# A decoder on one core: norm scaling, masks and feed-forward remainders open to a second elementwise engine, the diagonals' product in one piece per chunk, the softmax reciprocals as a task of their own

## The chip, the core and the metric

The kernel runs on one core of a Trainium2 chip. A core has five instruction queues, each of which is worked off strictly in order: PE (TensorE, matrix products and transposes), DVE (VectorE) and ACT (ScalarE) for elementwise work, POOL (GpSimd), which is used here for elementwise work and fills, and SP (SyncE), which issues all transfers. The metric is the device time of one execution in microseconds (us): 819.33 us is the median of three runs before the change (817.36 to 820.14).

## What is computed

Six layers, each followed by a layer norm of its sum with its input, over 8 batches of 256 tokens with 256 features, 16 heads of 16:

```python
x = ln(x + L0_attn(x))        # gated recurrence: z, h~, associative scan, gate
x = ln(x + L0_xattn(x, ctx, mask_ik1, bias))   # scores/4 + bias, -inf where mask == 0, softmax
x = ln(x + L0_ffn(x))         # norm, 8-bit grid over ALL batches, ternary weights
x = ln(x + L1_attn(x))        # relative positions: q.rel_k[idx], p.rel_v[idx], clipped at 20
x = ln(x + L1_xattn(ctx, ctx, x, mask_bk0))    # softmax over where(mask, q.k, -1e10)/4
x = ln(x + L1_ffn(x))         # silu(gate) * up, then down, 768 hidden

def ln(x):
    m = mean(x); v = var(x)
    return (x - m) / sqrt(v + 1e-5)
```

The maximum over all batches in `L0_ffn` is a barrier: no batch passes it before all have reached it.

## The kernel before

**A planner writes the queues.** Every step of the kernel is a Python generator that yields operations to `Order.run` (L139). An operation is made by `do(engine, cost, ready, emit)`, which fixes the engine, by `either(ready, (engine, cost, emit), ...)`, which offers several, or by `dma(...)`. The planner keeps a time for each engine at which it comes free, takes the operation that could start first (within 0.1 us the more urgent one), and emits its instructions. So the order of each queue is fixed when the program is built, out of the costs in the source, and on the chip each engine goes through its queue in that order. With `either`, the way that could start earliest is taken, and with equal starts the cheaper one: `copy` (PSUM to SBUF, DVE at 0.60 or ACT at 0.47) is the common case. PE's operations carry a kind: plain ("d"), scores ("s", four heads beside each other in row groups) and values ("v", four in column groups). Going from one kind to another has a price in the plan.

**Attention.** An item is one batch in one of three attentions: `x0` (L0_xattn), `s1` (L1_attn) and `x1` (L1_xattn). An item is worked in four quads of four heads. `quad` (L896) makes scores for four heads on PE, then for each head on DVE a custom instruction that adds the bias and finds the maximum (L941, `sn`, `nm`). `head` (L952) has ACT make the exponentials with their sums (L957, `p`), PE turn them (L502, `pt`), and DVE or ACT copy them out (L291 or L292, `pts`). `values` (L980) multiplies by the values on PE (L995, `pv`). After the fourth quad `attend_out` (L1015) does the rest in one string: reciprocals of the sums on DVE (L1020, `rsum`), their spread over the features on POOL (L1026, `rsw`), a turn on PE (`ps_rs`), a copy (`oT`), and for `s1` `by_distance` (L1443); then the product with `pv` (L1041), the output projection (`pso`), the residual (L1061) and the norm.

**Distances in s1.** Scores depend on the distance through a table that is written to DRAM and read back along diagonals as `band` (L1318 to L1357); the probabilities near the diagonal go to DRAM (`pb`) and come back as `acc` (L1425), one row per distance. `by_distance` turns `acc` on PE (L1455, `psa`), copies it (`at`) and adds its product with the value table into `pv` (L1468). It does so for two chunks `c` of features and two halves `t` of the tokens, each half with a turn, a copy and a product of its own, with two `at` buffers.

**Norms.** `norm` (L527) takes statistics on DVE (L538, L540), the reciprocal root on POOL (L543 to L548, `rs_...`) and the scaling, two instructions of 128x256, on DVE (L553, `x_...` and `xn`). `settle` and `turn_x` call it and turn the result for the next layer. There are 56 such scalings: 8 of l0a, which read PSUM, and 48 that read SBUF.

**Masks.** The x0 mask becomes `neg` on DVE (L1137) and is added into the bias on POOL (L1144); the x1 mask becomes `hide` on DVE (L1585).

**The last layer.** `gated` (L1657) makes gate and up products (`fg`, `fu`) in a rounded part and a remainder; for each third of the hidden features ACT makes the tanh (L1692), DVE two products (L1696, L1703), ACT the rounded copy `h[:, 0]` (L1708), and DVE the remainder `h[:, 1]` (L1712); then come the down product (L1723, `psd`), the residual (L1733), the norm and the output transfer.

**Loads.** `loads` (L367) puts the transfers of the beginning into SP's queue: `cols` (biases and norm scales), then `xT` of batch 0, the three recurrence weights `wa`, and so on.

Of the kernel before, what the change touches and what calls it, by code (L numbers as in the profile page):

```python
# [19 lines left out]
P = 128  # L20
# [176 lines left out]
def do(engine, cost, ready, emit, kind="d"):  # L197

    needs = [x for x in ready if isinstance(x, Held) and x.i is None]
    times = [x.at if isinstance(x, Held) else x for x in ready]  # L200
    return (yield ("op", [(engine, cost, emit)], max(times), kind, needs))
# [6 lines left out]
def dma(ready, count, emit, rate=300):  # L208

    return (yield ("op", [("SP", 0.0, emit)], max(ready), (count, rate), ()))  # L210
# [6 lines left out]
def get(slots, name, at=0.0):  # L217
    ((t, i),) = yield ("get", slots, 1, at)
    return Held(slots, name).take(t, i)
# [3 lines left out]
def kernel(  # L223
# [54 lines left out]
    def on_dve(n):  # L278
        return 0.08 + n * 1.02e-3
# [87 lines left out]
    def loads():  # L367
# [6 lines left out]
        t = yield from dma([0.0], 18432, lambda: nc.sync.dma_start(out=cols, in_=cols_in))  # L374
        yield from load_xT(0)
        for i in range(3):
            events["wa", i] = yield from dma(
                [0.0], 262144, lambda: nc.sync.dma_start(out=wa[i], in_=chunked(a_w[i]))
            )
        for b in range(1, 4):  # L380
            yield from load_xT(b)
# [145 lines left out]
    def norm(y, t_y, make, name, make2=None):  # L527
# [22 lines left out]
        def scaled(make, i):  # L550
            dst = make()
            for t in range(NQ):
                nc.vector.tensor_scalar(  # L553
                    dst[:, t, :], y[:, t, :], mv[:, t, 0:1], rstd[:, i, t : t + 1], ALU.subtract,
                    ALU.mult,
                )

        t = yield from do("DVE", 0.9, [t_y], stats)
        t_r = yield from do("POOL", 0.9 if n == 1 else 1.1, [t], root)
        if n == 2:  # L560
            t_2 = yield from do("DVE", 0.66, [t_r], lambda: scaled(make2, 1))
        t = yield from do("DVE", 0.66, [t_r], lambda: scaled(make, 0))
# [389 lines left out]
    def head(it, n, j, p, s, nm, t, left, times):  # L952
# [11 lines left out]
        it.t_sums.append(t_e)  # L964
        times.append(t_e)
# [49 lines left out]
    def attend_out(it, t_pv):  # L1015

        ai, b = it.ai, it.b
# [16 lines left out]
        oT = yield from get(oT_bufs, f"oT{it.name}", t)  # L1034
        t = yield from copy([t, oT.at], oT.tile, ps.tile)
        ps.drop(t)
        if ai == 1:
            t_pv = yield from it.by_distance(t_pv)
# [79 lines left out]
    def item_x0(b):  # L1118
# [3 lines left out]
        if b > 1:  # L1122
# [13 lines left out]
            "DVE", on_dve(512), [t_m, neg.at],  # L1136
            lambda: nc.vector.tensor_scalar(  # L1137
# [119 lines left out]
    def layer1_self():  # L1257
# [5 lines left out]
        at_bufs = slots(rel, "at", 2, [P, 4, P])  # L1263
# [22 lines left out]
    def item_s1(b, kr_bufs, wide_bufs, acc_bufs, tail_bufs, at_bufs, band_bufs):  # L1286
# [90 lines left out]
        def tails_task(n, p, left, t_p):  # L1377
# [43 lines left out]
            if len(it.t_pb) in (2, 4) and n % 2 == 1:  # L1421
# [14 lines left out]
                events[it.key("acc", c)] = t_d  # L1436
                if c == 1:
                    it.pb_set.drop(t_d)
# [4 lines left out]
        def by_distance(t_pv):  # L1443
            for c in range(KC):
                t_a = yield from event(it.key("acc", c))
                for n in (2 * c, 2 * c + 1):
                    t_t = yield from event(it.key("tail", n))
                    t_a = max(t_a, t_t)
                for t in range(NQ):
                    ps = Held(banks, f"psa{b}_{t}_{c}")  # L1450
                    turned = lambda: ps.tile.rearrange("p a (j q) -> p (a j) q", q=P)

                    def emit():
                        for j in range(4):
                            nc.tensor.transpose(  # L1455
                                turned()[: 2 * NA, j, :],
                                it.acc.tile[:, c, t, 2 * j : 2 * j + 2, :].rearrange("p h r -> p (h r)"),
                                ident,
                            )

                    t_t = yield from do("PE", TURNS, [t_a, ps], emit)
                    at = yield from get(at_bufs, f"at{b}_{t}_{c}", t_t)
                    t_t = yield from copy([t_t, at.at], at.tile[: 2 * NA], turned()[: 2 * NA])
                    ps.drop(t_t)

                    def emit():
                        for j in range(4):
                            nc.tensor.matmul(  # L1468
                                it.pv.tile[32 * j : 32 * j + 32, c, t * P : (t + 1) * P],
                                drv[:, t, :],  # L1470
                                at.tile[: 2 * NA, j, :],
                                start=False,
                                stop=(t == NQ - 1 and c == KC - 1),
                                tile_position=(0, 32 * j),
                                skip_group_check=True,
                            )

                    t_pv = yield from do("PE", on_pe(256), [t_t, t_pv], emit, "v")
                    at.drop(t_pv)
            it.acc.drop(t_pv)  # L1480
            return t_pv

        it.by_distance = by_distance
# [84 lines left out]
    def item_x1(b):  # L1568
# [3 lines left out]
        if b > 0:  # L1572
# [11 lines left out]
            "DVE", on_dve(512), [t_m, hide.at],  # L1584
            lambda: nc.vector.tensor_scalar(  # L1585
# [71 lines left out]
    def gated(b, gu, dn, t_w, hT_bufs):  # L1657
# [13 lines left out]
        for i in range(NH // 2):  # L1671
            psg = Held(banks, f"fg{b}_{i}")

            def emit(ps, w):
# [35 lines left out]
            t = yield from do(  # L1710
                "DVE", on_dve(512), [t],
                lambda: nc.vector.tensor_tensor(h[:, 1], sg.tile, h[:, 0], ALU.subtract),  # L1712
# [135 lines left out]
```

## Time and profile before

| | before |
|---|---|
| median of 3 runs (range) | 819.33 us (817.36 to 820.14) |
| the profiled execution, device time | 817.66 us |
| its span, first to last instruction | 815.9 us |
| instructions | 21213 |
| matrix products on PE, weight loads | 7175, 7175 |
| mean granted TensorE clock | 0.995 |
| moved by the transfers | 77.67 MB, mean 95 GB/s |

The profile shows one execution. Its page gives the busy time of each engine, 40 slices of the span with the busy share of each engine in tenths, the chain of work that ended last, and groups of equal instructions by source line. Further views list the engines' busy time in chosen stretches ("windows"), who waited for whom, and the instructions in order of time. A PE matrix product overlaps its neighbours, so PE counts as busy while it is not at its best pace. In the order of time the stages are: the recurrence to about 60 us, x0 to about 280 us, the barrier and L0_ffn with the start of s1 to about 320 us, s1 with x1 beside it to about 690 us, and the last layer with the remaining x1 items to the end.

### The profile page before, as it was taken

To read this page: it belongs to the slowest core of one execution; us is meant where nothing else is said; L and a number is where in the kernel's file an instruction comes from. 1 tells how busy PE (TensorE), PEld (TensorE's weight loads), DVE (VectorE), ACT (ScalarE), POOL (GpSimd) and SP (SyncE) were. 2 spreads that over 40 slices of the span, in tenths; PEclk is the share of its full clock that TensorE was granted. 3 is DMA by queue.
4 is the path that set the end of the run, shared out by engine and by line. 5 is a ranking of instruction groups with operands and counts; after the bars stand their busy time and mean duration, and the time that the engine had idled before them with its cause. 6 is when DMAs were issued, how large, how long until landed. Compare 5 with 4: busy or idle time off the path is not lost.

```text
span 815.9 us, 21213 instructions
## 1 busy us (share of the span) xinstructions
PE 782.6 (96%) x7175; PEld 598.8 (73%) x7175; DVE 700.7 (86%) x2452; ACT 635.4 (78%) x2047; POOL 209.9 (26%) x398
## 2 busy tenths in 40 slices
PE   7999999999999999999999999999999999999995
PEld 6886777776777786656666777776777766799884
DVE  3899889988888698787899799899898998989985
ACT  2349988989988458896789799899899898846841
POOL 3520221121211044234333213242243322110020
PEclk9999999999999999999999999999999999999997
DMA  5735521100100449899976406645357443000001
GB/s 181 224 114 84 70 46 44 39 16 27 41 27 28 155 101 216 165 170 185 173 158 137 112 26 133 133 93 120 88 112 155 108 100 100 19 28 14 15 14 39
DMA packets 177681, 77.67 MB, mean 95 GB/s; under 512 B 155046, under 2 KB 171430, under 8 KB 177574
## 3 DMA queue, kind: packets, MB, share of 16 engines
q1 hardware_dynamic: 177574, 76.32, 41.9%
q8 instruction: 57, 0.93, 0.5%
q14 instruction: 50, 0.41, 0.2%
HBM read 41.66 MB, written 34.64 MB: 94 GB/s over the span
## 4 chain that ended last, share of the span: by engine, by line
PE 62%; DVE 13%; ACT 10%; DMA 6%; issue 4%; POOL 2%; SPq 2%; POOLq 0%; DVEq 0%; ACTq 0%
PE pt L502 14%; PE s L913 9%; PE pv L995 8%; ACT p L957 7%; PE pso L519 4%; DVE sn L941 4%; PE psv L519 4%; PE psq L508 4%; PE psk L508 3%; PE psd L1723 3%; ACT pts L292 2%; PE psa L1455 2%; DMA sk<-w 1%; PE fg L1678 1%; PE psr L1308 1%
## 5 line engine op out<-in xcount | busy, mean ns | idle before, releaser
L957 ACT ACTIVATE p<-sn,nm 128x256 f32<-128x256 f32 x768 | 381.3, 507 | 23.9 <-DVE nm L941 18.4
L502 PE MATMUL pt<-ident,p 128*128 128x128 f32 x1536 | 207.1, 277 | 5.2 <-ACT p L957 2.1
L502 PEld LDWEIGHTS pt<-ident,p 128*128 128x128 f32 x1536 | 169.4, 140 | 47.3 <-ACT p L957 24.7
L292 ACT COPY pts<-pt 128x512 f32<-128x512 f32 x274 | 147.7, 586 | 20.7 <-PE pt L502 19.8
L957 ACT ACTIVATION_READ_ACCUMULATOR p<-sn,nm 128x1 f32 x768 | 151.6, 197 | 0.0
L913 PE MATMUL s<-k,q 32*128 32x256 f32 (+2 forms) x1792 | 122.2, 371 | 2.6 <-DVE nm L941 1.2
L995 PE MATMUL pv<-pts,v 128*32 128x256 f32 x1536 | 107.4, 385 | 0.6 <-ACT pts L292 0.5
L941 DVE CUSTOM_DVE_ANT_0 sn<-s,band 128x256 f32<-128x256 f32 x256 | 93.9, 417 | 14.1 <-ACT p L957 6.3
L941 DVE CUSTOM_DVE_ANT_0 sn<-s,bias 128x256 f32<-128x256 f32 x256 | 93.8, 418 | 12.6 <-PE s L913 7.1
L941 DVE CUSTOM_DVE_ANT_0 sn<-s,hide 128x256 f32<-128x256 f32 x256 | 93.2, 417 | 12.9 <-PE s L913 10.6
L913 PEld LDWEIGHTS s<-k,q 32*128 32x128 f32 x1792 | 78.5, 184 | 34.2 <-issue 21.5
L291 DVE COPY pts<-pt 128x512 f32<-128x512 f32 x110 | 73.9, 683 | 4.5 <-PE pt L502 3.5
L995 PEld LDWEIGHTS pv<-pts,v 128*32 128x32 f32 x1536 | 42.9, 109 | 43.9 <-issue 19.8
L941 DVE DVE_READ_ACCUMULATOR2_ANT nm<- 128x1 f32 x768 | 62.8, 82 | 0.0
L519 PE MATMUL pso<-wvo,oT 128*128 128x256 f32 x192 | 47.1, 388 | 1.5 <-DVE oT L1041 1.5
L1026 POOL COPY rsw<-rsum 128x512 f32<-128x512 f32 x24 | 14.6, 610 | 126.2 <-DVE rsum L1020 99.0
L519 PEld LDWEIGHTS pso<-wvo,oT 128*128 128x128 f32 x192 | 34.8, 190 | 11.1 <-issue 3.2
L1318 POOL COPY w<-w 128x504 f32<-128x504 f32 x32 | 19.3, 603 | 87.8 <-DVE w L291 47.2
L1417 DVE TENSOR_REDUCE acc<-tail 128x8 f32<-128x864 f32 x32 | 33.4, 1043 | 3.0 <-POOL tail L1406 3.0
L1345 POOL COPY band<-ends 64x256 f32<-64x256 f32 x64 | 21.4, 360 | 47.1 <-DVE nm L941 47.0
L519 PE MATMUL psv<-wvo,ctxT 128*128 128x256 f32 x128 | 30.5, 381 | 0.3 <-DVE xnT L1093 0.3
L508 PE MATMUL psk<-ctxT,wqk 128*128 128x256 f32 x128 | 30.4, 381 | 0.0
(197 smaller groups left out, 1310.2 us busy)
## 6 DMA issues: line engine op xcount, KB each, us to landing
sk<-w SPq DMA_DIRECT2D x32, 416.0 KB
band<-sk SPq DMA_DIRECT2D x64, 104.0 KB
pb<-p SPq DMA_DIRECT2D x64, 104.0 KB
band<-sk SPq DMA_DIRECT2D x64, 84.0 KB
pb<-p SPq DMA_DIRECT2D x64, 84.0 KB
acc<-pb SPq DMA_DIRECT2D x32, 156.0 KB
ctxT<-in_ctxT SPq DMA_DIRECT2D x16, 256.0 KB
wpad<-in_qk_w SPq DMA_DIRECT2D x6, 512.0 KB
```

The costliest lines, as they stand in the source:

```text
L291: ("DVE", on_dve(n), lambda: nc.vector.tensor_copy(dst, src)),
L292: ("ACT", on_act(n), lambda: nc.scalar.copy(dst, src)),
L502: nc.tensor.transpose(ps[:, c, t * P : (t + 1) * P], src[:, t, c * P : (c + 1) * P], ident)
L508: nc.tensor.matmul(ps, w[:, c, lo:hi], rhs[:, c, :], start=(c == 0), stop=(c == KC - 1))
L519: nc.tensor.matmul(ps[:, t, :], srcT[:, c, t * P : (t + 1) * P], w[:, c, :], start=(c == 0), stop=(c == KC - 1),)
L913: nc.tensor.matmul(ps[j].tile[:, t, first : first + w], it.q.tile[32 * j : 32 * j + 32, c, t * P : (t + 1) * P], k[32 * j : 32 * j + 32, c ...
L941: nc.vector.tensor_tensor_reduce(out=s.tile[:, t, :], in0=ps[j].tile[:, t, :], in1=tile[:, t, :], scale=-1.0, scalar=3e38, op0=ALU.add, op ...
L957: nc.scalar.activation(p.tile[:, j, q, :], s.tile[:, q, :], AF.Exp, bias=nm[:, q : q + 1], scale=-1.0, accum_out=it.sum_of(q, h),)
L995: nc.tensor.matmul(it.pv.tile[32 * j : 32 * j + 32, c, :], it.v.tile[:, k, head_of(n, j), :], pts.tile[:, k, :], start=(k == 0 and i == 0 ...
L1345: nc.gpsimd.tensor_copy(band.tile[0:BLK, :, t, lo:hi], it.ends[c][0:BLK, t, i:HH:2].unsqueeze(2).to_broadcast([BLK, 4, hi - lo]),)
L1417: lambda: nc.vector.tensor_reduce(acc[:, c, :, own, 1], tail.tile, AX.X, ALU.add),
L1723: nc.tensor.matmul(ps.tile[:, t, :], hT.tile[:, r, m, t * P : (t + 1) * P], dn[:, m, :], start=(m == 0 and r == 0), stop=(m == NH - 1 and ...
```

## The change

Six edits are made at once.

1. In `norm`, the scaling (now `both`) is offered to DVE at 0.66 or to POOL at 1.7, but for l0a, which stays on DVE.
2. The masks' `neg` and `hide` are made on POOL, at 0.6.
3. The remainder `h[:, 1]` of the last layer is offered to DVE (0.60) or to POOL at 1.3.
4. `scales` is split off `attend_out`: reciprocals, spread, turn and copy are a task that starts with the last exponential of the item, at the urgency of its last quad; `attend_out` waits for it by an event.
5. `by_distance` becomes `distances(c)`: for each chunk two turns and two copies, then one product over both halves. It starts when `acc` of chunk 0 is on its way, and no longer after the values. `at` is one buffer of twice the size instead of two.
6. The load of `cols` moves behind `xT` of batch 0 and the first recurrence weight.

As built, 48 scaling instructions (24 pairs: 7 of `xn`, 1 of `x_l0x`, 4 of `x_l0f`, 3 of `x_l1a`, 4 of `x_l1x`, 5 of `x_l1f`), 16 mask instructions and 9 of the 24 remainders stand in POOL's queue; PE has the same 7175 products in another order. The planner also deals some copies and additions anew between DVE and ACT.

```diff
-        t = yield from dma([0.0], 18432, lambda: nc.sync.dma_start(out=cols, in_=cols_in))
         yield from load_xT(0)
...
             )
+            if i == 0:
+                yield from dma([0.0], 18432, lambda: nc.sync.dma_start(out=cols, in_=cols_in))
         for b in range(1, 4):
...
-        def scaled(make, i):
-            dst = make()
+        def scaled(engine, dst, i):
             for t in range(NQ):
-                nc.vector.tensor_scalar(
+                engine.tensor_scalar(
                     dst[:, t, :], y[:, t, :], mv[:, t, 0:1], rstd[:, i, t : t + 1], ALU.subtract,
...
                 )
+
+        def both(t, dst, i):
+            if name.startswith("l0a"):
+                return do("DVE", 0.66, [t], lambda: scaled(nc.vector, dst, i))
+            return either(
+                [t],
+                ("DVE", 0.66, lambda: scaled(nc.vector, dst, i)),
+                ("POOL", 1.7, lambda: scaled(nc.gpsimd, dst, i)),
+            )
...
         if n == 2:
-            t_2 = yield from do("DVE", 0.66, [t_r], lambda: scaled(make2, 1))
-        t = yield from do("DVE", 0.66, [t_r], lambda: scaled(make, 0))
+            t_2 = yield from both(t_r, make2(), 1)
+        t = yield from both(t_r, make(), 0)
         return t if n == 1 else (t, t_2)
...
         it.t_sums.append(t_e)
+        if len(it.t_sums) == H:
+            order.spawn(urgency(it, NS - 1), scales(it))
         times.append(t_e)
...
-    def attend_out(it, t_pv):
-
-        ai, b = it.ai, it.b
+    def scales(it):
+
         rs = small.tile([P, NQ, H], F32, tag="rsum", name=f"rsum{it.name}")
...
         wide.drop(t)
-        oT = yield from get(oT_bufs, f"oT{it.name}", t)
+        oT = it.oT = yield from get(oT_bufs, f"oT{it.name}", t)
         t = yield from copy([t, oT.at], oT.tile, ps.tile)
         ps.drop(t)
+        events[it.key("scales")] = t
+
+    def attend_out(it, t_pv):
+
+        ai, b = it.ai, it.b
+        t = yield from event(it.key("scales"))
+        oT = it.oT
         if ai == 1:
-            t_pv = yield from it.by_distance(t_pv)
+            t_pv = yield from event(it.key("distances"))
         t = yield from do(
...
         t = yield from do(
-            "DVE", on_dve(512), [t_m, neg.at],
-            lambda: nc.vector.tensor_scalar(
+            "POOL", 0.6, [t_m, neg.at],
+            lambda: nc.gpsimd.tensor_scalar(
                 neg.tile, mask.tile, 0.0, NEG_INF, ALU.is_equal, ALU.mult
...
         tail_bufs = slots(rel, "tail", 1, [P, NQ, 4, P - MR])
-        at_bufs = slots(rel, "at", 2, [P, 4, P])
+        at_bufs = slots(rel, "at", 1, [P, NQ, 4, P])
...
                 events[it.key("acc", c)] = t_d
+                if c == 0:
+                    order.spawn(urgency(it, NS - 1), distances(0))
                 if c == 1:
...
-        def by_distance(t_pv):
-            for c in range(KC):
-                t_a = yield from event(it.key("acc", c))
-                for n in (2 * c, 2 * c + 1):
-                    t_t = yield from event(it.key("tail", n))
-                    t_a = max(t_a, t_t)
+        def distances(c):
+
+            t_a = yield from event(it.key("acc", c))
+            for n in (2 * c, 2 * c + 1):
+                t_t = yield from event(it.key("tail", n))
+                t_a = max(t_a, t_t)
+            at = yield from get(at_bufs, f"at{b}_{c}", t_a)
+            times = []
+            for t in range(NQ):
+                ps = Held(banks, f"psa{b}_{t}_{c}")
+                turned = lambda: ps.tile.rearrange("p a (j q) -> p (a j) q", q=P)
+
+                def emit():
+                    for j in range(4):
+                        nc.tensor.transpose(
+                            turned()[: 2 * NA, j, :],
+                            it.acc.tile[:, c, t, 2 * j : 2 * j + 2, :].rearrange("p h r -> p (h r)"),
+                            ident,
+                        )
+
+                t_t = yield from do("PE", TURNS, [t_a, ps], emit)
+                t_t = yield from copy([t_t, at.at], at.tile[: 2 * NA, t], turned()[: 2 * NA])
+                ps.drop(t_t)
+                times.append(t_t)
+            t_v = yield from event(it.key("values", 2 * c + 1))
+
+            def emit():
                 for t in range(NQ):
-                    ps = Held(banks, f"psa{b}_{t}_{c}")
-                    turned = lambda: ps.tile.rearrange("p a (j q) -> p (a j) q", q=P)
-
-                    def emit():
-                        for j in range(4):
-                            nc.tensor.transpose(
-                                turned()[: 2 * NA, j, :],
-                                it.acc.tile[:, c, t, 2 * j : 2 * j + 2, :].rearrange("p h r -> p (h r)"),
-                                ident,
-                            )
-
-                    t_t = yield from do("PE", TURNS, [t_a, ps], emit)
-                    at = yield from get(at_bufs, f"at{b}_{t}_{c}", t_t)
-                    t_t = yield from copy([t_t, at.at], at.tile[: 2 * NA], turned()[: 2 * NA])
-                    ps.drop(t_t)
-
-                    def emit():
-                        for j in range(4):
-                            nc.tensor.matmul(
-                                it.pv.tile[32 * j : 32 * j + 32, c, t * P : (t + 1) * P],
-                                drv[:, t, :],
-                                at.tile[: 2 * NA, j, :],
-                                start=False,
-                                stop=(t == NQ - 1 and c == KC - 1),
-                                tile_position=(0, 32 * j),
-                                skip_group_check=True,
-                            )
-
-                    t_pv = yield from do("PE", on_pe(256), [t_t, t_pv], emit, "v")
-                    at.drop(t_pv)
-            it.acc.drop(t_pv)
-            return t_pv
-
-        it.by_distance = by_distance
+                    for j in range(4):
+                        nc.tensor.matmul(
+                            it.pv.tile[32 * j : 32 * j + 32, c, t * P : (t + 1) * P],
+                            drv[:, t, :],
+                            at.tile[: 2 * NA, t, j, :],
+                            start=False,
+                            stop=(t == NQ - 1 and c == KC - 1),
+                            tile_position=(0, 32 * j),
+                            skip_group_check=True,
+                        )
+
+            t_v = yield from do("PE", on_pe(512), [t_v, *times], emit, "v")
+            at.drop(t_v)
+            if c + 1 < KC:
+                yield from distances(c + 1)
+                return
+            it.acc.drop(t_v)
+            events[it.key("distances")] = t_v
+
...
         t_h = yield from do(
-            "DVE", on_dve(512), [t_m, hide.at],
-            lambda: nc.vector.tensor_scalar(
+            "POOL", 0.6, [t_m, hide.at],
+            lambda: nc.gpsimd.tensor_scalar(
                 hide.tile, mask.tile, 0.0, NEG_INF, ALU.is_equal, ALU.mult
...
             )
-            t = yield from do(
-                "DVE", on_dve(512), [t],
-                lambda: nc.vector.tensor_tensor(h[:, 1], sg.tile, h[:, 0], ALU.subtract),
+            t = yield from either(
+                [t],
+                ("DVE", on_dve(512), lambda: nc.vector.tensor_tensor(h[:, 1], sg.tile, h[:, 0], ALU.subtract)),
+                ("POOL", 1.3, lambda: nc.gpsimd.tensor_tensor(h[:, 1], sg.tile, h[:, 0], ALU.subtract)),
             )
```

## The prediction

> **What bounds the kernel now.** I read the page's busy times and slices first, then the busy times in stretches, then the chain of waits, then single stretches in order of time.
>
> ```profile
> span 815.9 us, 21213 instructions
> PE 782.6 (96%) x7175; PEld 598.8 (73%) x7175; DVE 700.7 (86%) x2452; ACT 635.4 (78%) x2047; POOL 209.9 (26%) x398
> ...
> PE 62%; DVE 13%; ACT 10%; DMA 6%; issue 4%; POOL 2%; SPq 2%; POOLq 0%; DVEq 0%; ACTq 0%
> ```
>
> ```profile
> 80.00:120.00 40.00, 39.09 (x356) 29.51 (x354) 35.88 (x134) 37.10 (x123) 8.81 (x12) 1.00 0.47 72
> ...
> 320.00:360.00 40.00, 38.31 (x379) 26.90 (x379) 31.21 (x117) 36.99 (x126) 13.15 (x32) 1.00 0.91 184
> 480.00:520.00 40.00, 39.65 (x423) 28.91 (x421) 37.15 (x143) 38.69 (x136) 11.61 (x24) 1.00 0.48 104
> 720.00:760.00 40.00, 40.00 (x347) 36.82 (x345) 36.40 (x99) 23.20 (x62) 6.30 (x12) 1.00 0.06 21
> ```
>
> (Columns: stretch, length, then busy us of PE, PE's weight load, DVE, ACT, POOL with instruction counts, granted clock, DMA share, GB/s.) PE looks full, but its busy time contains waiting inside the pipeline. So I priced its work at the best pace that the chain of waits shows: 24 transposes in 2.62 us, 8 products of a projection in 1.73, 16 of scores in 1.08, 16 of values in 1.00, 24 of the down product in 2.88, and 0.118 us for one of gate or up. With the counts of the groups this makes 723 us. The span is 815.9, so some 93 us are lost on PE: 9 in the first 40 us, 20 in 40 to 280, 24 in 280 to 440 (the transfers are near full there: share 0.91), 20 in 440 to 680, 9 in 680 to 800, 10 in the tail. The 723 can't be touched by this change; only the 93 can. In 720:760 almost nothing is lost (97% of the pace). In 80 to 280 and 440 to 680 DVE and ACT are about 90% busy beside a PE at 91 to 92% of its pace: three engines that hand work round in fixed order, each waiting a little for the others.
>
> **Relief of DVE (edits 1, 2, 3).** 24 of the 48 scaling pairs that read SBUF stand in POOL's queue. What a pair costs DVE, and what it costs when POOL is in its way, one stretch in order of time shows (start, length, engine, line):
>
> ```profile
> 726.02 0.74 DVE L553 TENSOR_SCALAR x_l1f<-yf,mv_l1f,rs_l1f 128x256 f32<-128x256 f32 x2 [1.10 <-POOL rs_l1f L548]
> 726.67 0.69 DVE L1733 SCALAR_TENSOR_TENSOR yf<-psd,x_l1x 128x512 f32<-128x512 f32 x1
> ...
> 729.67 1.75 DVE L553 TENSOR_SCALAR x_l1f<-yf,mv_l1f,rs_l1f 128x256 f32<-128x256 f32 x2
> ```
>
> ```profile
> 729.94 1.33 POOL L1049 TENSOR_TENSOR xb<-x_l1a,rows 128x512 f32<-128x512 f32 x1
> ```
>
> The next instruction starts 0.65 us after the pair, so a pair is 0.65: 24 x 0.65 = 15.6 us off DVE. A pair that meets POOL's addition takes 1.75. The excess of the means over the medians of the five groups (for instance 573 against 408 ns for `x_l1x`) is about 6 us over 80 instructions; half of them go, so 3 us. Masks: 16 x 0.42 (median) = 6.7, and one `hide` that took 1.49 gives back another 1.1. Remainders: 9 x 0.60 (0.69, but the next starts 0.60 later) = 5.4. Sum 31.8, say 31 us of DVE's 701. As built, the planner then gives DVE more copies and takes about 6 us off ACT; that is the same relief, shared.
>
> How much of 31 us reaches the end? DVE is one of three engines in the circle and 13% of the chain. The moved lines alone (`x_...`, `xn`, `hT`) are about 13 us of that chain, added up over its pieces. But where DVE steps back, PE or ACT is next, and they are at 90%. I take a third, **10 us**; the ends are 0 (PE takes it all) and 24 (half of the loss in 40 to 280 and 440 to 680, and some beside it).
>
> **What POOL's pairs cost.** No row shows POOL scaling with an operand per partition. Two rows are near, and a third by its two inputs:
>
> ```profile
> L683 POOL TENSOR_SCALAR a<-z 128x512 f32<-128x512 f32 x8 | 5.3, 666 | 12.1 <-ACT z L674 11.4 <-DVE h L705 0.7
> L687 POOL TENSOR_SCALAR z<-z 128x512 f32<-128x512 f32 x8 | 4.9, 618 | 0.6
> ...
> L1049 POOL TENSOR_TENSOR xb<-x_l0f,rows 128x512 f32<-128x512 f32 x8 | 10.2, 1272 | 0.0
> ```
>
> By `a` and `z` a pair (2 x 256 elements) is at least 0.65 to 0.8; by the addition 1.3; the plan's own price is 1.7. The other POOL prices of the plan stand within some 15% of their rows (the addition 1.3 against 1.28, the spread 0.58 against 0.61), so I take 1.7 and keep 0.8 as the other end. POOL's busy time then grows by 24 x 1.7 + 16 x 0.62 (row `z`) + 9 x 1.28 = 62 us, to about 272 of 816. It has the room, but it is a queue in order: behind a scaling or a mask stand roots of norms, `rsw`, fills of `band` and `w`, and the tails. A pair on POOL comes 1.05 later than on DVE. 19 of the 24 are followed by a turn on PE (all but `x_l1f`, though `x_l0x` waits for the barrier). The plan placed these turns with 1.7 in view, so only what it misjudged counts: I charge **2 us** (0 to 8). The `neg` on POOL waits for the mask's transfer, with `bias` and the root of the batch before behind it; before, POOL's `bias` waited for `neg` all the same (21.4 us over six waits in the list of waits), so I cost it at nothing. `hide` has `band` fills behind it, which feed a transfer that DVE's score instruction needs; POOL's `w` copies wait 88 us in all for others there, that is the cover. Without it, each late mask would cost its own lateness.
>
> [...] By the trace: of about 168 such DVE instructions before (scaling, masks, `k<-kin`, remainders, quantising), with POOL 26% busy, the visible excess was 7.5 us. About 95 of them stay, with POOL 33% busy: 7.5 x 95/168 x 33/26 = 5.4. [...]
>
> **The diagonals (5).** PE pays for going to and fro between kinds of product. Eight distance products take 0.36 us when they stand alone (before `psa`) and 0.24 beside value products (420.57 to 420.81):
>
> ```profile
> 420.57 0.43 PE L1468 MATMUL pv<-at,drv 82*32 82x128 f32 x8
> 420.81 1.05 PE L995 MATMUL pv<-pts,v 128*32 128x256 f32 x16
> ...
> 468.99 0.43 PE L1468 MATMUL pv<-at,drv 82*32 82x128 f32 x8
> 469.35 0.63 PE L1455 MATMUL psa<-ident,acc 128*82 128x128 f32 x4
> ```
>
> 16 pieces fewer: 16 x 0.12 = **2 us**. PE waits now some 3.5 us for `at` copies before these products; the second copy of a chunk still ends last, so I take nothing. Chunk 0's turns now stand before the last quad's. Its transfer was issued at 341.7 to 343.2 for the first item and used at 357.3; some groups earlier still leaves several us, against 3.6 to 4.9 on the chain at 422.
>
> **Early reciprocals (4).** `rsum`, `rsw`, `ps_rs` and `oT` move ahead of the last values. DVE waited 4.4 us for `oT` copies and distance products before L1041 in all, of which the relief already contains part: **1 us** (0 to 3). It holds an `oT` buffer longer; both items have one.
>
> **The load (6).** `cols` takes 0.46 us of SP before `xT`; moved back, the first product may start 0.46 earlier. But the chain then runs through the weight transfers and 24 small issues to 24.9 us, which stay: nothing (0 to 0.5). Its reader `hb` must be ready at 8.76; it was ready at 3.3, and one more us is covered.
>
> **Sum.** 10 - 2 + 2 + 1 = 11 us off the profiled execution's own 817.66 (815.9 of span and 1.8 around it), 806.7. The median of the runs shown is 1.7 higher, 819.33 - 11 = 808.3. I say **808**.
>
> **The rivals.** *PE takes it.* If PE is the bound in earnest, as in 720:760, DVE's relief only lengthens DVE's waits; the 3 us of diagonals and reciprocals less 2 stay: about 818, up to 815 with a small part of the relief. For it: PE 96% busy, the same 7175 products, the chain 62% PE. Against it: 93 us below pace. *POOL is late.* One mechanism: a scaling on POOL takes longer than the plan's 1.7, and PE, in order, stands before the turn that needs it. If a pair takes 2.7, 19 turns come 1 us late, with nothing in front that can go ahead: 19 us against a gain of 13, about 825; it decides from a pair of about 2.4 on. For it: no row shows this form; [...] POOL roots sit in the same queue. Against it: the plan's other prices hold. *It isn't done:* the queues as built show 24 pairs, 16 masks and 9 remainders on POOL, so this is out.
>
> **How the numbers follow.** Forecast (about 800 to 815): 0.5; PE takes it (815 to 820): 0.22; POOL late (820 to 832): 0.28. The range 797 to 827 leaves out a tenth at each end or less; the likeliest case alone is 800 to 815. 0.3% is about what a measurement of this kernel can tell from no change: 816.9 to 821.8. Of the second case half lies below it and half within: faster 0.60, same 0.12, slower 0.28.
>
> **What would show it.** Right: DVE busy at about 675, POOL at about 270, POOL pairs at 1.6 to 1.8, PE idle and lost time in 40 to 280 and 440 to 680 down by some 10 us, no long DVE scalings. Wrong: PE waits for `x_l0f`, `x_l1a`, `x_l1x` or `xn` on POOL above a few us; POOL pairs above 2.4; or an unchanged loss on PE with DVE idle.

## The result and the profile after

| | before | after |
|---|---|---|
| median of 5 runs (range), same chip | 819.33 us (817.36 to 821.86) | 826.52 us (825.56 to 828.47) |
| ratio, 95% interval | 1 | 1.0088 (1.0067 to 1.011) |
| the profiled execution, device time | 817.66 us | 826.42 us |
| its span | 815.9 us | 824.6 us |

The changed kernel is slower by 0.9%, some 7 us; 808 was predicted, with 797 to 827 as the range. The page of the changed kernel, its span, busy times and shares of the chain of waits:

```profile
span 824.6 us, 21205 instructions
...
PE 781.1 (95%) x7175; PEld 597.8 (72%) x7175; DVE 682.1 (83%) x2384; ACT 630.0 (76%) x2035; POOL 315.9 (38%) x470
...
PE 55%; ACT 16%; DVE 13%; POOL 7%; issue 4%; DMA 4%; SPq 1%; POOLq 0%; DVEq 0%; ACTq 0%
```

DVE lost 18.6 us of work and POOL gained 106, where 62 had been summed. In the chain of waits POOL's share went from 2% to 7%, ACT's from 10% to 16% and PE's from 62% to 55%. What became so long on POOL, its groups of instructions with shapes kept apart show (count, busy us, mean ns of one, idle before):

```profile
L553 POOL TENSOR_SCALAR xn<-xb,mv_l0x,rs_l0x 128x256 f32<-128x256 f32 x14 | 17.9, 1285 | 0.8
L1610 POOL TENSOR_SCALAR hide<-mask 128x512 f32<-128x512 uint8 x8 | 15.6, 1955 | 16.4 <-DMA mask<-in_mask 16.1
L1154 POOL TENSOR_SCALAR neg<-mask 128x512 f32<-128x512 int32 x8 | 15.5, 1939 | 0.7
...
L1738 POOL TENSOR_TENSOR hT<-sg,hT 128x512 fp32r<-128x512 f32 x9 | 11.6, 1288 | 29.2 <-ACT hT L1733 29.2
...
L553 POOL TENSOR_SCALAR x_l0f<-yf,mv_l0f,rs_l0f 128x256 f32<-128x256 f32 x8 | 10.3, 1293 | 0.4
```

A scaling pair is 2 x 1.29 = 2.6 us (2.5 in the mean of all 24), not the plan's 1.7; a mask 1.95, not 0.6; only the remainder (1.29) is what the sum had. What PE waited for in the changed kernel (engine, line, releaser: us in total, times, longest):

```profile
PE pt L503 <- ACT p L966: 6.9, 15, 2.6
PE psz L509 <- DMA wa<-in_a_w: 4.5, 1, 4.5
PE ps_xn L503 <- POOL xn L553: 4.3, 6, 0.9
PE ps_l0f L503 <- POOL x_l0f L553: 4.0, 5, 1.0
PE pt L503 <- DVE nm L950: 3.7, 7, 1.4
```

The same view of before:

```profile
PE pt L502 <- ACT p L957: 2.1, 9, 0.7
PE pso L519 <- DVE oT L1041: 1.5, 2, 0.9
PE pv L1468 <- ACT at L292: 1.5, 4, 0.7
...
PE ps_xn L502 <- DVE xn L553: 1.3, 3, 0.5
...
PE pt L502 <- DVE nm L941: 1.0, 2, 0.6
PE ps_l0f L502 <- DVE x_l0f L553: 1.0, 2, 0.7
```

Two kinds of wait have grown. Before turns of `xn` and `x_l0f` PE stood 2.3 us, for DVE, and stands 8.3 us now, for POOL (and 0.9 still for DVE). Before turns of `p` it stands 7.5 us more (6.9 + 3.7 against 2.1 and 1.0 for the same two releasers). The waits for `oT` and `at` are no longer among those above 0.5 us.

When the stages end (start of the last instruction of a kind on PE, in the one profiled execution of each kernel) says where the time came in:

| us | last turn at the barrier (`ps_gmax`) | last `psf` of L0_ffn | last `psr` of s1 | last `ps_l1a` turn | last `psd` |
|---|---|---|---|---|---|
| before | 279.0 | 301.9 | 625.5 | 685.6 | 808.7 |
| after | 281.5 | 307.5 | 631.1 | 693.9 | 817.0 |
| difference | 2.5 | 5.6 | 5.6 | 8.3 | 8.3 |

In this pair of executions two thirds arise before 308 us, in the stages whose norms are `xn` and `x_l0f`. The busy times in stretches show it too (columns as in the prediction), before first:

```profile
280.00:320.00 40.00, 37.35 (x248) 29.47 (x246) 37.18 (x113) 24.76 (x58) 16.19 (x40) 1.00 0.67 137
```

```profile
280.00:320.00 40.00, 34.71 (x202) 27.69 (x200) 32.78 (x86) 20.43 (x38) 24.36 (x40) 1.00 0.56 140
320.00:360.00 40.00, 36.13 (x354) 24.79 (x354) 28.43 (x111) 30.26 (x105) 11.83 (x30) 0.96 0.88 177
...
720.00:760.00 40.00, 39.99 (x358) 37.23 (x358) 35.12 (x100) 28.39 (x79) 16.78 (x19) 1.00 0.04 15
```

In 280:320 of the changed kernel every engine but POOL did less, and PE got through 202 products instead of 248 (its stretch begins earlier in the work, since the barrier is 2.5 us later, and the products are in part others, so the counts alone prove little). PE's standing there before turns of `x_l0f` is the whole 4.0 us for POOL; before, the same turns cost 1.0 us of waiting for DVE. One place of it in order of time, first PE, then POOL:

```profile
291.26 0.60 PE L520 MATMUL psf<-wq,xq 128*128 128x256 bf16 x4
292.48 0.33 PE L503 MATMUL ps_l0f<-ident,x_l0f 128*128 128x128 f32 x1 [0.62 <-POOL x_l0f L553]
293.69 0.55 PE L503 MATMUL ps_l0f<-ident,x_l0f 128*128 128x128 f32 x3 [0.88 <-POOL x_l0f L553]
294.07 3.62 PE L509 MATMUL psq<-xT_l0f,wqk 128*128 128x256 f32 x16
```

```profile
289.96 0.95 POOL L549 TENSOR_TENSOR rs_l0f<-rs_l0f,half 128x2 f32<-128x2 f32 x1
291.01 2.62 POOL L553 TENSOR_SCALAR x_l0f<-yf,mv_l0f,rs_l0f 128x256 f32<-128x256 f32 x2
```

PE stands twice inside one pair, once for each half, until POOL is done at 293.63 (291.01 + 2.62).

### The profile page after: what moved, and what is told of

Its sections match the earlier page's. It is cut to its first block, busy times and chain, and to the rows that moved or that the text cites. A ratio compares the mean times of both kernels' runs of the same rounds, so it can differ in the third digit from the quotient of the medians.

```text
span 824.6 us, 21205 instructions
## 1 busy us (share of the span) xinstructions
PE 781.1 (95%) x7175; PEld 597.8 (72%) x7175; DVE 682.1 (83%) x2384; ACT 630.0 (76%) x2035; POOL 315.9 (38%) x470
## 4 chain that ended last, share of the span: by engine, by line
PE 55%; ACT 16%; DVE 13%; POOL 7%; issue 4%; DMA 4%; SPq 1%; POOLq 0%; DVEq 0%; ACTq 0%
PE pt L503 12%; ACT p L966 11%; PE s L922 7%; PE pv L1006 7%; DVE sn L950 4%; ACT pts L292 3%; PE psq L509 3%; PE pso L520 3%; PE psk L509 3%; PE psv L520 3%; PE psd L1749 3%; POOL xn L553 2%; PE psz L509 2%; PE psh L509 1%; PE psg L509 1%
## 5 line engine op out<-in xcount | busy, mean ns | idle before, releaser
L503 PE MATMUL pt<-ident,p 128*128 128x128 f32 x1536 | 210.2, 278 | 12.0 <-ACT p L966 6.9
L292 ACT COPY pts<-pt 128x512 f32<-128x512 f32 x270 | 145.3, 587 | 26.5 <-PE pt L503 24.4
L922 PE MATMUL s<-k,q 32*128 32x256 f32 (+2 forms) x1792 | 118.1, 369 | 0.5 <-ACT p L966 0.3
L291 DVE COPY pts<-pt 128x512 f32<-128x512 f32 x114 | 77.0, 683 | 8.4 <-PE pt L503 7.6
```

The source lines that it names most:

```text
L291: ("DVE", on_dve(n), lambda: nc.vector.tensor_copy(dst, src)),
L292: ("ACT", on_act(n), lambda: nc.scalar.copy(dst, src)),
L503: nc.tensor.transpose(ps[:, c, t * P : (t + 1) * P], src[:, t, c * P : (c + 1) * P], ident)
L922: nc.tensor.matmul(ps[j].tile[:, t, first : first + w], it.q.tile[32 * j : 32 * j + 32, c, t * P : (t + 1) * P], k[32 * j : 32 * j + 32, c ...
```

## The experiments

Three theories: (1) the slow scaling on POOL makes PE stand; (2) another order of the queues, not any single cost, made the time; (3) the slow masks did. Each ratio is to the kernel before on the same chip (its median there was 822.74 us in one comparison and 827.35 to 827.63 in the others), so ratios are compared, not microseconds.

### Taking the parts back, or shortening them

`norms_dve`, all scaling on DVE:

```diff
-            if name.startswith("l0a"):
+            if True:
```

> The changed kernel with the norms' scaling back on DVE; masks, remainders, diagonals and reciprocals as changed. Theory 1 (the scalings on POOL come later than the plan has them, and PE stands before their turns): most of the 7 us go, 817 to 821, ratio to before 0.997 to 1.002. Theory 2 (the loss is in the new order of PE, from diagonals and reciprocals, whoever scales): 825 to 828. Theory 3 (the masks, at three times their price and waiting for transfers in POOL's queue): 824 to 828.

`masks_dve`: in both mask steps `"POOL", 0.6` becomes `"DVE", on_dve(512)` and `nc.gpsimd` becomes `nc.vector`.

> The changed kernel with the two masks back on DVE, the rest as changed. Theory 1 (scalings): 824 to 828. Theory 2 (order): 825 to 828. Theory 3 (masks): 815 to 820.

`short_scaling`, the order of the changed kernel with a scaling on POOL that leaves the norm out:

```diff
+                if engine is nc.gpsimd:
+                    engine.tensor_scalar(dst[:, t, :], y[:, t, :], 0.5, 0.0, ALU.mult, ALU.add)
+                    continue
```

> The changed kernel with the same order in all queues, but each scaling on POOL takes two constants instead of mean and deviation, so that those 24 pairs leave the norm out (they halve their input). By the rows of the recurrence such a pair should take about 0.8 us instead of 2.5. Theory 1 (scalings late): 808 to 817. Theory 2 (order): 825 to 828, since the order is the same. Theory 3 (masks): 823 to 828.

`true_prices`: the plan's prices on POOL, 1.7 to 2.5 for a pair and 0.6 to 2.0 for a mask.

> The changed kernel with the plan told what POOL takes: 2.5 for a scaling and 2.0 for a mask instead of 1.7 and 0.6; the instructions are the same, their order is planned anew. Theory 1: the plan puts other work before the late turns, 815 to 822. Theory 2 (order): no reason for a gain, 822 to 830. Theory 3 (masks): 818 to 824, since the masks' followers are placed rightly but the waits for transfers stay.

`elementwise_dve`: scaling, masks and remainders all on DVE; diagonals, reciprocals and the load stay as changed. `changed_again`: the changed kernel once more.

> The changed kernel with scaling, masks and remainders all back on DVE: only diagonals, reciprocals and the place of one load are changed. Theory 1 (scalings on POOL late) leaves the order a small gain, as the norms on DVE alone had: ratio 0.993 to 1.000. Theory 2 (the order costs): 1.004 to 1.010. If the masks on POOL are themselves a gain, as the masks back on DVE at 1.014 could mean, this one is slower than the norms on DVE alone (0.993) by 0.3% or more.

> The changed kernel once more, beside the others of this comparison, since the kernel before took 827.6 on the chip of the first four experiments and 819.3 on the first one. All theories: ratio to before 1.006 to 1.011.

| kernel | ratio (95%) |
|---|---|
| `norms_dve` | 0.9934 (0.9914 to 0.9954) |
| `masks_dve` | 1.0139 (1.0105 to 1.0172) |
| `short_scaling` | 0.9929 (0.9907 to 0.995) |
| `true_prices` | 1.0092 (1.006 to 1.0124) |
| `elementwise_dve` | 1.0048 (1.003 to 1.0066) |
| `changed_again` | 1.0061 (1.0037 to 1.0085) |

`short_scaling` has the instructions of every queue in the changed kernel's order, so its 1.3 to 1.6% against the changed kernel (1.0061 to 1.0091 in three comparisons) is due to the 24 pairs: to their length, or to the mean and deviation that they no longer read, which a run below tells apart. The others build a new order, and two of them don't add up: with everything back on DVE the ratio is 1.005, with the norms alone back 0.993. A plan that knows the true prices doesn't help: it still gives 26 pairs to POOL, since `either` takes the earliest start and doesn't ask for the end. Taking masks off POOL came out slower, outside the range of all three theories.

### Which form is slow

`pool_forms`: the kernel before with nine more instructions of 128x256 on POOL at its start, one after the other, with different operations and operands.

> The kernel before with nine instructions of 128x256 added in POOL's idle time at the start, whose results nobody reads: two constants with product and sum, with difference and product, with comparison and product; two operands per partition with product and sum, with difference and product; one operand per partition; one constant; and product and sum, comparison and product on integers. Theory 1a (operands per partition are slow): constants 0.36, operands 1.2. Theory 1b (difference and comparison are slow, product and sum fast): product and sum 0.36 in both kinds, the others above 0.9. The total is no measurement here.

The order of time on POOL:

```profile
3.92 0.41 POOL L368 TENSOR_SCALAR form<-blocks 128x256 f32<-128x256 f32 x1
4.28 1.09 POOL L368 TENSOR_SCALAR form<-blocks 128x256 f32<-128x256 f32 x1
5.34 1.08 POOL L368 TENSOR_SCALAR form<-blocks 128x256 f32<-128x256 f32 x1
6.42 0.55 POOL L368 TENSOR_SCALAR form<-blocks,ones 128x256 f32<-128x256 f32 x1
6.95 1.22 POOL L368 TENSOR_SCALAR form<-blocks,ones 128x256 f32<-128x256 f32 x1
8.16 0.94 POOL L366 TENSOR_SCALAR form<-blocks,ones 128x256 f32<-128x256 f32 x1
9.07 0.85 POOL L366 TENSOR_SCALAR form<-blocks 128x256 f32<-128x256 f32 x1
9.89 0.41 POOL L368 TENSOR_SCALAR form<-mi 128x256 f32<-128x256 int32 x1
10.26 1.08 POOL L368 TENSOR_SCALAR form<-mi 128x256 f32<-128x256 int32 x1
```

In this order: constants with product and sum 0.41, with difference and product 1.09, with comparison and product 1.08; operands per partition with product and sum 0.55, with difference and product 1.22; a product alone, by an operand 0.94, by a constant 0.85; integers with product and sum 0.41, with comparison and product 1.08. Each is a single instruction. So it is mainly the pair of operations that sets the time. Operands per partition add 0.09 to 0.14, integers nothing. Rows `a` and `z`, from which the prediction took its lower ends, are products with a sum; neither the norm nor the mask was of that form.

### The masks alone

In both masks:

```diff
-                neg.tile, mask.tile, 0.0, NEG_INF, ALU.is_equal, ALU.mult
+                neg.tile, mask.tile, -NEG_INF, NEG_INF, ALU.mult, ALU.add
```

`mask_sum` does this in the changed kernel's order, `norms_dve_mask_sum` in that of `norms_dve`.

> The changed kernel in its own order, with the masks on POOL as mask x 1e30 - 1e30 (the same numbers): 0.65 us instead of 1.94. Theory 1 (scalings late): 1.004 to 1.009, hardly better than the changed kernel. Theory 3 (masks late): 0.995 to 1.002. The norms on DVE with short masks were 0.1% under the norms on DVE with long ones, so I expect little.

> The changed kernel with the norms on DVE, and the masks on POOL as mask x 1e30 - 1e30 (the same numbers, from a product and a sum) instead of a comparison and a product; the order of all queues is that of the norms on DVE alone. If the mask's length of 1.94 us comes from the comparison, it falls to about 0.65, and the time to 0.990 to 0.993 of before; if from reading integers, both stay.

`mask_sum` gave 1.0068 (1.0049 to 1.0087), `norms_dve_mask_sum` 0.9924 (0.9903 to 0.9945). A mask took 0.62 to 0.68 us in them instead of 1.94 to 1.98, and either result lies within 0.3% of its counterpart with the long masks: 1.0061 to 1.0091 for the changed kernel in three comparisons, 0.9934 for `norms_dve`. Theory 3 falls.

### The norm as product and sum, in one order

`sums_same_order` computes the norm on POOL as y x r + (-m x r), in the changed kernel's own order:

```diff
+            if engine is nc.gpsimd:
+                off = small.tile([P, NQ], F32, tag="ln_off", name=f"off{i}_{name}")
+                engine.tensor_tensor(off, rstd[:, i], mv[:, :, 0], ALU.mult)
+                engine.tensor_scalar(off, off, -1.0, 0.0, ALU.mult, ALU.add)
+                for t in range(NQ):
+                    engine.tensor_scalar(
+                        dst[:, t, :], y[:, t, :], rstd[:, i, t : t + 1], off[:, t : t + 1],
+                        ALU.mult, ALU.add,
+                    )
+                return
```

`sums_early` does so only for the 12 pairs of layer 0 (`xn`, `x_l0x`, `x_l0f`), `sums_late` only for the 12 of layer 1. `changed_third` is the changed kernel on the same chip. `both_sums` has the short masks too and was compared with the kernel before on another chip. In the traces of all five PE's 7175, DVE's 2384 and ACT's 2035 instructions stand in the same order.

> The changed kernel in its own order, scalings on POOL as y x r + (-m x r) (product and sum), masks as changed; nothing is left out. Theory 1 (length of the POOL scalings): 0.991 to 0.996, at least 1% under the changed kernel beside it. If the short scalings gained by leaving mean and deviation out: as the changed kernel.

> As the run before, but with the short form only for the norms of the first three layers on POOL (7 xn, 1 x_l0x, 4 x_l0f), which stand before the barrier and before the first transfers of the distances. Theory 1a (the length counts where PE has no other work: x0's end and L0_ffn): nearly all of the gain, 0.991 to 0.998. Theory 1b (it counts everywhere alike, 12 of 24 pairs): half, 0.998 to 1.003.

> The short form only for the other 12 pairs (3 x_l1a, 4 x_l1x, 5 x_l1f). Theory 1a: as the changed kernel, 1.003 to 1.010. Theory 1b: half of the gain, 0.998 to 1.003.

> The changed kernel beside the three that follow, all with one order in PE's, DVE's, ACT's and SP's queue. Ratio to before 1.004 to 1.010.

> The changed kernel in its own order with scalings and masks on POOL as product and sum. The scalings alone gave 0.997 in this order and the masks alone 1.007 against 1.009: 0.994 to 0.998.

| kernel | short pairs | ratio (95%) | barrier | last `psf` | last `psd` |
|---|---|---|---|---|---|
| `changed_third` | none | 1.0091 (1.0076 to 1.0106) | 284.1 | 310.1 | 826.6 |
| `sums_late` | 12 of layer 1 | 1.0069 (1.0054 to 1.0083) | 281.0 | 307.0 | 821.1 |
| `sums_early` | 12 of layer 0 | 0.9986 (0.9968 to 1.0003) | 276.7 | 300.9 | 819.8 |
| `sums_same_order` | all 24 | 0.9971 (0.9958 to 0.9984) | 276.3 | 300.5 | 813.7 |
| `both_sums` | all 24, and masks | 0.9965 (0.9948 to 0.9982) | 277.4 | 301.6 | 811.4 |

The groups of the short form in `sums_same_order`:

```profile
L557 POOL TENSOR_SCALAR xn<-xb,rs_l0x,off_l0x 128x256 f32<-128x256 f32 x14 | 7.7, 559 | 0.7
...
L554 POOL TENSOR_TENSOR off_l0x<-rs_l0x,mv_l0x 128x2 f32<-128x2 f32 x8 | 1.6, 198 | 0.6
...
L555 POOL TENSOR_SCALAR off_l0x<-off_l0x 128x2 f32<-128x2 f32 x8 | 1.5, 193 | 0.7
```

A pair now takes 1.5 to 1.7 us, two small steps included (2 x 0.56 + 0.20 + 0.19 for `xn`), 1.0 less than before in the mean. This alone moves the ratio from 1.0091 to 0.9971, by 1.2% or 9 to 10 us (the medians are 833.86 and 825.27), and nearly all of it is due to the early 12. Mean and deviation are still read, so it is the length that counts. `sums_same_order` and `sums_early` came out just above the ranges expected of them.

The last three columns are of one execution each, and they scatter. The turn at the barrier stands between 281.0 and 284.4 us in five executions with the changed order and long early pairs; in the two with the highest value (284.1 in `changed_third`, 284.4 in `mask_sum`) PE's granted clock was 0.66 in 30:35, where it was 1.00 in the others. In the four executions with short early pairs it stands between 276.3 and 277.4, clear of that scatter. `sums_late`, with 281.0, is the fairer neighbour for the early columns, and the 6 us between the last `psd` of `sums_early` and `sums_same_order` are not borne out by their ratios, which differ by 0.15%.

The place shown above, in `sums_same_order`:

```profile
286.10 0.60 PE L520 MATMUL psf<-wq,xq 128*128 128x256 bf16 x4
287.22 0.33 PE L503 MATMUL ps_l0f<-ident,x_l0f 128*128 128x128 f32 x1 [0.52 <-POOL x_l0f L557]
287.76 0.55 PE L503 MATMUL ps_l0f<-ident,x_l0f 128*128 128x128 f32 x3 [0.21 <-POOL x_l0f L557]
288.15 3.62 PE L509 MATMUL psq<-xT_l0f,wqk 128*128 128x256 f32 x16
```

Before the second half PE stands 0.21 us, where it stood 0.88. In this place PE gains about 0.8 us (the `psq` behind the turn starts 2.05 us after the `psf` product ahead of it, where it was 2.81: 286.10 to 288.15 and 291.26 to 294.07); such places add up. The list of waits of `sums_same_order` has left of the 8.3 us:

```profile
PE ps_l0f L503 <- POOL x_l0f L557: 1.4, 4, 0.5
...
PE ps_xn L503 <- POOL xn L557: 0.2, 1, 0.2
```

So 6.7 of the 9 to 10 us are PE's direct standing; where the other 2 to 3 us lie isn't shown. They are not relief of DVE by shorter work on POOL: DVE is busy for 680.7 us in `changed_third` and 679.7 in `sums_same_order`. Theory 1, the length of POOL's pairs, is what made the change slow.

### What an order alone does, and other plans

`order_window` is the kernel before with the planner's window at 0.12 instead of 0.1 us; `order_act` has ACT priced 0.01 us higher per instruction.

> The kernel before with the plan's window of 0.1 us (within which the more urgent operation goes first) at 0.12: the same instructions in another order. It shows how much a new order alone moves the time. If orders are worth little: 0.997 to 1.003; if chance in the order is as large as what the single edits seem to be worth: beyond 0.5% from 1.

> The kernel before with ACT's price in the plan 0.01 us higher for each operation: nearly the same instructions, another order. Expected as for the window.

`sums_on_pool` has both short forms and plans with 1.6 for a pair. `by_end` gives POOL an operation only where it would end no later than on DVE:

```diff
+                ends = {e: max(self.free[e], ready) + c for e, c, _ in ways}
                 for engine, cost, emit in ways:
+                    if engine == "POOL" and ends[engine] > min(ends.values()):
+                        continue
```

> The changed kernel with both POOL forms as product and sum: masks as above, scalings as y x r + (-m x r), with two small instructions for -m x r ahead; the plan's price of a pair is 1.6. By the added forms a pair takes 1.1, with the small ones 1.5 to 1.9. Theory 1 (length of the scalings): 0.990 to 0.996, as the short scalings. If what counts is the instruction left out (mean and deviation) and not the length: 1.004 to 1.009.

> As the run before, but the plan offers POOL an operation only where POOL would end it no later than DVE, not where it would start it first; POOL then has 3 scalings and 1 remainder left, and the order is new. If giving DVE's work to POOL is a gain in itself: slower than the run before. If only the masks and the order were the gain: 0.990 to 0.996, as with the norms on DVE.

`order_window` gave 1.0027 (1.0014 to 1.004), `order_act` 1.0084 (1.0056 to 1.0112), `sums_on_pool` 0.9924 (0.9901 to 0.9948), `by_end` 1.0036 (1.0021 to 1.0052). The first two do the work of before with hardly another price in the plan, and are 0.3 and 0.8% slower. So a difference of this size between two orders can't be put down to the edit that led to the new order, and `masks_dve`, `elementwise_dve` and `by_end` decide nothing. Theory 2 is a real source of time, but it can't be the cause in `sums_same_order`, which has the changed kernel's order. The fastest versions are `sums_on_pool` and `norms_dve_mask_sum`, 0.9924 each.

## Why the prediction was wrong

**The step that failed** is "What POOL's pairs cost". It put a pair between 0.8 (rows `a`, `z`) and 1.7 (the plan's price), took 1.7 because the plan's other POOL prices agreed with their rows, and charged 2 us (0 to 8). The pair measures 2.5 to 2.6. Taking 1.0 us off each brought 9 to 10 us, so the 0.8 us beyond the plan are worth some 8 us (an estimate by proportion). At about the plan's length the charge would have held: with pairs of 1.5 to 1.7 PE's standing before turns of `xn` and `x_l0f` is 1.6 us. The agreement of the other prices was no evidence: they belong to other operations. The upper end of 1.7 was not a bound either, since no row of before had difference and product on POOL. The rival "POOL is late" named the mechanism and the place (in order, before turns), and its point, 2.4, was passed. It put the time at 825 from 19 turns of 1 us; direct standing is 9.1 us (`xn`, `x_l0f`, and 0.8 for `x_l1a`), and the late layer-1 pairs cost little, so its sum was right only in size. The sum forecast a gain of 11 us where 7 were lost. Of these 18 us the pairs explain 8 to 10; the rest is the next term.

**Relief of DVE, 10 us.** DVE's busy time fell to 682.1 instead of 675. What the relief is worth shows where the pair keeps the plan's price: `both_sums`, with pairs of 1.5 to 1.7 and masks of 0.62, gives 0.9965, about 3 us instead of the 11 of the sum, with diagonals and reciprocals in it. With a pair near the lower end, 0.8 (`short_scaling`), it is 0.9929, about 6. This term was too large, or was given back, or the new order happened to be a slow one: an order alone moved the kernel before by 0.3 and 0.8%, 2 to 7 us. One place where it may have been given back stands in the changed kernel after the barrier; in order of time ACT, then PE:

```profile
340.76 0.51 ACT L966 ACTIVATE p<-sn,nm 128x256 f32<-128x256 f32 x1 [3.72 <-DMA pb<-p]
```

```profile
341.41 0.33 PE L503 MATMUL pt<-ident,p 128*128 128x128 f32 x1 [2.57 <-ACT p L966]
```

ACT waits for a `p` buffer whose transfer to DRAM isn't done, PE for ACT. In `changed_third`, `sums_early`, `sums_same_order` and `both_sums` the same stall of PE is 3.9 to 4.6 us, and there ACT waits for `band` (5.1 to 5.7 us). The kernel before, `norms_dve` and `norms_dve_mask_sum` have no stall above 1.2 us on PE between 320 and 360. All nine executions in the changed kernel's order have it, with 2.6 to 5.6 us, so the length of a pair doesn't remove it. It stands in the stage where the transfers are near full (share 0.88). With the clock lost after it (below) the stall makes 4 to 9 us as a plain sum, and the kernels before and after take the same 323.6 us from the last `psf` to the last `psr`, so any gain there was lost again in the same stage. That it takes the relief's missing 8 us was not tried by itself.

**The masks** were priced at 0.62 from row `z` and are 1.95. That they cost nothing held all the same: the short form changes 0.3% at most.

**Long scalings on DVE** were expected to become fewer. Some are left (an `x_l1f` of 1366 ns, 781.71 to 783.08, beside POOL's addition from 781.60 to 782.92; the median is 411). Their excess over 407 ns each was to fall from about 6 us to 3; it is still about 5 over the 48 instructions left. All 16 of them that took more than 470 ns overlap an instruction on POOL, and so did all 10 before; but of the 32 shorter ones 20 overlap one too, so not every meeting costs time. DVE's work fell by 18.6 us in all.

**Diagonals and reciprocals.** The waits that they were to remove are gone (1.5 us each on PE in the list of before). Whether they bring 3 us can't be told: `elementwise_dve`, which has them without the relief, is 0.5% slower than before in an order of its own.

**The load** did what was said: the first product starts at 4.48 instead of 4.97, and nothing of it shows after 40 us: PE was busy for 33.8 us of them, and for 34.0 before. `hb` came at 6.3 instead of 3.3, still ahead of its reader at 8.27.

What stays open: whether the missing relief is the stall, the chance of the order or a term set too large, and why the step from `psr` to `ps_l1a` adds 2.7 us, which the length of the late pairs doesn't explain.

## What to carry to other kernels

Before an elementwise step moves to another engine, measure that very form there, both operations of it: a near row with another pair of operations can be wrong by a factor of three (here 0.41 against 1.08 us, and 0.62 against 1.95). In a queue written out ahead, an engine that can start first but ends later is no help where an in-order consumer stands right behind it (PE stood 8.3 us before turns of `xn` and `x_l0f`); look at the end, and put the slow engine on steps with slack (layer 1 bore its 12 long pairs for 0.2%). Where a plan makes the order, compare in one order, for the order alone moved this kernel by up to 0.8%.

## What the hardware showed besides

**POOL's one fast form.** Of the pairs tried, product and sum alone is fast (0.41 us; difference or comparison with a product 1.08 to 1.09): even a product by itself (0.85 us) takes twice as long as the product with a sum added (0.41).

**The clock after a stall.** Behind the stall above, which ends at 341.41, the granted clock is half for a while. Windows of 5 us of the changed kernel:

```profile
340.00:345.00 5.00, 3.26 (x24) 1.64 (x24) 2.07 (x6) 4.24 (x15) 1.71 (x4) 0.80 0.62 123
345.00:350.00 5.00, 5.00 (x49) 3.65 (x42) 1.14 (x4) 1.60 (x6) 0.00 (x0) 0.86 0.76 137
```

In finer steps it is 0.50 from about 343.0 to 346.4: 3.4 us, so 1.7 us of clock lost. Sixteen products of values take 1.94 us there (at 343.67) and 1.07 at full clock (at 336.31). Thirteen stalls of PE of 2.41 to 5.59 us were found between 320 and 440 us, in the traces of thirteen kernels. Each has half clock in it or behind it, six times for about 3.4 us and seven times for about 6.8. Of four shorter ones, of 1.74 to 2.27 us, one has it (1.92 us, in `order_window`). The length of a stall alone doesn't settle it: behind a stall of 1.17 us at `psy` the clock is 0.66 in 30:35 of `changed_third`, and behind one of the same length it is 1.00 there in the changed kernel. What halves it isn't shown. The profile of before has such a dip only in its tail (0.77 in 805:810), at a place where PE is done but for the last products. With the lost clock added, a stall of PE can thus be dearer than its length: here 2.6 us and 1.7, elsewhere up to 5.6 us and 3.4 (estimates, as plain sums).

**The chip.** One and the same kernel before had medians of 819.33 to 827.63 us in the comparisons, more than the effect studied; only ratios within a comparison carry.
